# Seven filter outputs a block on all rows, and layer 0's convolution steps placed earlier, in a two-layer graph network kernel

## The chip, the cores and the metric

The kernel runs on one core of one Trainium2 chip. The metric is the device time of one execution in microseconds (us), as the median of several runs. "Span" below is the time from the first to the last instruction of the one execution that the profiler recorded.

## What is computed

For 64 graphs of 256 nodes with 256 features (all fp32), two layers run one after the other. Layer 0 has a convolution branch along the nodes, a message branch over the graph, and gates that mix both; layer 1 is a normalised aggregation.

```python
# layer 0, per graph
h = relu(bn1(conv1d(x^T, conv1_w, width 1)))
h = bn2(conv1d(h, conv2_w, width 17, pad 8))        # 256 -> 256 channels, 17 taps
x_conv = relu(h + x^T)^T
s = x @ w_se^T + b_se                                # 3 features
A = exp(-|s_n - s_m|^2) * adj
x_nmp = A @ relu(x @ w_msg^T + b_msg)
r, z, n = GRU gates of [x_conv, x_nmp] and x         # w_ih, w_hh
x = layernorm(x + (1 - z) * n + z * x)
# layer 1
h = layernorm(x) * gamma + beta
x = layernorm(x + x + relu((adj @ h) @ W_rel + b_rel + h @ W_root))
```

## The kernel before, in words

**Transform of the 17-tap convolution.** The node axis of a graph is cut into 16 stretches of 16, and two neighbouring stretches make a transform of length 32. VectorE (DVE in the profile) does the transforms as trees of two-input operations on the big tile `XF` (`fold` L789, `split` L607, `butterflies` L701, `merge` L640). Between them stands one complex product per frequency, done with three real 256x256 matrices on TensorE (PE). So the filter is needed as 47 real matrices (`NM`) of 256x256 instead of 17 taps.

**Filters (L523 to L592).** Those 47 matrices are made on the chip, once. The taps come from DRAM in pieces (`wt`, two buffers, L545). GpSimd (POOL) gathers the taps of a few outputs into a tile `ws` (L555, four buffers), TensorE turns it over (L562), ScalarE (ACT) copies the result out of PSUM to `tT` (L564), TensorE multiplies it with a constant matrix `taps` (L584), and ScalarE copies the product to its place in `W2` (L592). Before the change one block holds 3 outputs: 3 x 17 taps = 51 rows, product 128x141 (3 x 47). Two blocks lie one above the other in `ws` and `tT`, in rows 0 to 50 and 64 to 114, and the two products of such a pair use the two halves of the array's rows. A round has 6 blocks; there are 30 rounds, two of them with 2 blocks. That makes 172 products and 86 transposes, 60 gathers and 60 copies to `W2`.

**Batches and pairs.** The 64 graphs are 8 batches of 8. `conv1(b)` (L800) does for batch b, two graphs at a time, the load of x, its transposes (L841), the width-1 convolution (L862), and for b > 0 the store of the result to DRAM (`hd`, L871). `conv(b)` (L873) loads it back (L876), folds it (L795), splits it, does the products (`products`, L731; for b > 0 the matrices come from DRAM into the double-buffered `cs`, L724), merges, and leaves the convolved rows in `XC`. `pair(p)` (L1087) takes two graphs: messages (L1110), distances (L1143), aggregation (L1157), gates (L1195 for the first two pairs and the last one, L1209 with fewer products for the others), then the norm, projection (L1356) and aggregation (L1370) of layer 1, and the store.

**What sets the order.** All instructions are first recorded with a due time (`key`). `scheduled` (L316) then lays them out with a model of each engine's durations: at each step the ready instruction with the smallest key goes next on its engine. Keys of a pair count from `FIRST_GATES + p * PERIOD`; `spread` (L458) deals the steps of `filters`, `conv` and `conv1` evenly over a stretch of keys given by constants: `AHEAD_FROM, AHEAD_TO` for `conv1(1)`, `CONV1_FROM, CONV1_TO` for later `conv1`, `CONV_FROM, CONV_OUT, CONV_TO` for `conv`, `FILTERS_TO` for the filters. `PAIR_LEAD` makes the gates' DVE work more urgent than the convolution's. The keys only decide an order: on the chip each engine runs its own list in that order and waits by semaphores. All DMAs of the main part are issued by the SP queue, also in that order, so one that waits holds back those after it.

Of the kernel before, what the change touches and what calls it, by code (L numbers as in the profile page):

```python
# [18 lines left out]
P = 128  # L19
B, N, D = 64, 256, 256  # L20
C = D // P
TAPS, PAD = 17, 8
# [29 lines left out]
NM = 3 * len(LEAVES) + 2  # L52
SR, LR = 32, 100
SQ = 32
OB, OG = 3, 64
HQ = 2 * M * C * (M + 1)
XC_SLOTS = BG + 2
FIRST_GATES, PERIOD, GATE_TIME = 126, 59.2, 17.0
AHEAD_FROM, AHEAD_TO, W_DEEP = -20.0, 10.0, 2
CONV1_FROM, CONV1_TO, CONV_FROM, CONV_OUT, CONV_TO = -10.0, 120.0, -6.0, -58.0, -30.0  # L60
PAIR_LEAD, FILTER_LEAD, LOAD_AHEAD = 20.0, 15.0, 16.4
SMALL_RUNS, TURN_FROM = 1.3, 3
FILTERS_TO, STORES_AT = 50.0, 55.0
KEEP = 8.0
W_FROM, W_LAG = 2, 17.4
PLAIN, SUMS_FROM = (0, 1, B // 2 - 1), 2


# [101 lines left out]
class Op:  # L170

    def __init__(self):
        self.engine, self.calls, self.dur, self.moved, self.urgent = None, [], 0.0, 0, 0.0
        self.pre, self.post, self.spaces = set(), [], []


def one_line(line):
# [5 lines left out]
class Program:  # L183
# [13 lines left out]
    def add(self, name, method, args, named, line, reads, writes, dur, moved=0):  # L197
        op = self.joined
        if op is None or op.engine is None:
            op = op or Op()  # L200
            op.engine, op.key, op.seq = ENGINES[name], self.key, len(self.ops)
            self.key += self.step
            op.urgent = self.lead if op.engine == "DVE" else 0.0
            self.ops.append(op)
        op.calls.append((name, method, args, named, line))
        op.dur += dur
        op.moved += moved
        self.depend(op, reads, writes)
        return op

# [57 lines left out]
class Engine:  # L268
# [4 lines left out]
    def __getattr__(self, method):  # L273
        program, name = self.program, self.name

        def call(*args, hold=(), need=(), lines_up=0, **named):
# [12 lines left out]
            if method == "dma_start":  # L289
                v = outs[0] if isinstance(outs[0], View) else named["in_"]  # L290
                dur, moved = 0.06, v.size() * v.at.shape[0] * 4
                if program.joined is not None:
                    moved *= SMALL_RUNS
            elif name == "tensor":
# [21 lines left out]
def scheduled(ops):  # L316
# [4 lines left out]
    banks, held, queue = [0.0] * BANKS, {}, {}  # L321
    use, dma = dict.fromkeys(SHARES, 0), 0.0
    for op in ops:
        op.left, op.est = len(op.pre), op.key if op.engine == "SP" else 0.0
        for q in op.pre:
            q.post.append(op)
        for s in op.spaces:
            if s.where == "psum" and s.real is None and op.seq == s.ops[0].seq:
                s.left = {o.seq for o in s.ops}
                if s.line:  # L330
                    queue.setdefault(s.line, deque()).append(s)
# [83 lines left out]
def gnn_two_layers(  # L415
# [18 lines left out]
    prog = Program()  # L434
# [47 lines left out]
    xt_dram = tc.dram_tile([B // 2, P, C, 2 * N], F32, name="xt")  # L482
    w_dram = tc.dram_tile([2, SQ, 2 * C * C, P // SQ, P], F32, name="wd")
    W2 = sb("w2all", [P, C, NM, D], "first")
    taps = sb("taps", [P, NM * OB], "filters")

    prog.at(0.0)
    A.dma_start(out=chan_sb, in_=chan)
    A.dma_start(out=w1, in_=w1T.rearrange("(c p) n -> p c n", p=P))
    tb = np.zeros((2, OG, NM * OB), np.float32)  # L490
    tb[:, :TAPS * OB] = np.einsum("kf,op->kofp", tap_matrix(), np.eye(OB, dtype=np.float32)).reshape(TAPS * OB, NM * OB)
    tb = tb.reshape(P, NM * OB)
    A.dma_start(out=taps, in_=nc.inline_tensor(np.ascontiguousarray(tb), name="tap_matrix").ap())
    V.memset(mhalf, -0.5)
    V.memset(ones, 1.0)
# [25 lines left out]
            SP.dma_start(out=w2m[f:g, c].rearrange("f p o -> p f o"), in_=W2[:, c, f:g, :])  # L521

    def filters():  # L523
        pieces, rounds = [], []
        for c in range(C):
            for o0, o1 in ((0, 30 * OB), (30 * OB, 60 * OB), (60 * OB, D)):
                for o in range(o0, o1 - 6 * OB + 1, 6 * OB):
                    rounds.append((len(pieces), o, 3))
                if o1 == D:
                    rounds.append((len(pieces), D - 2 * OB, 1))  # L530
                pieces.append((c, o0, o1))
        WT, TT = {}, {}
        WS, AHEAD = {}, 4
        wts = ring("wt", [P, TAPS, 30 * OB], 2, "filters")
        wss = ring("ws", [P, 3, 2, OG], AHEAD, "filters")
        tTs = ring("tT", [P, 3, P], 2, "filters")
        for _ in range(AHEAD):
            G.memset(next(wss), 0.0)

        def fetch(i):  # L540
            if i < len(pieces):
                c, o0, o1 = pieces[i]
                t = next(wts).rearrange("p k o -> p (k o)")[:, :TAPS * (o1 - o0)]
                WT[i] = t.rearrange("p (k o) -> p k o", k=TAPS)
                SP.dma_start(out=WT[i], in_=w2T[c, :, :, o0:o1])  # L545

        def laid(i):
            piece, o, n = rounds[i]
            o -= pieces[piece][1]
            if i == 0 or rounds[i - 1][0] != piece:  # L550
                fetch(piece + 1)
            WS[i] = next(wss)
            for g in range(2):
                at = o + g * n * OB
                G.tensor_copy(WS[i][:, :n, g, :TAPS * OB].rearrange("p b (k o) -> p b k o", o=OB),  # L555
                              WT[piece][:, :, at:at + n * OB].rearrange("p k (b o) -> p b k o", o=OB))

        def turned(i):
            ps, n = bank("ps_tT"), rounds[i][2]
            with prog.group():  # L560
                for k in range(n):
                    PE.transpose(ps[:, k * P:(k + 1) * P], WS[i][:, k].rearrange("p g e -> p (g e)"), ident)  # L562
            tT = next(tTs)
            A.copy(tT[:, :n].rearrange("k b p -> k (b p)"), ps[:, :n * P])  # L564
            return tT

        fetch(0)
        for i in range(AHEAD):
            laid(i)
        TT[0] = turned(0)  # L570
        done = 0
        for i, (piece, o, n) in enumerate(rounds):
            c = pieces[piece][0]
            done = done if o else 0
            if i + AHEAD < len(rounds):
                laid(i + AHEAD)
            if i + 1 < len(rounds):
                TT[i + 1] = turned(i + 1)
            pss, size = [bank("ps_w") for _ in range(2)], NM * OB
            with prog.group():  # L580
                for k in range(n):
                    for g in range(2):
                        r = slice(g * OG, g * OG + TAPS * OB)
                        PE.matmul(pss[g][:, k * size:(k + 1) * size], TT[i][r, k, :], taps[r, :], start=k == 0,  # L584
                                  stop=k == n - 1, skip_group_check=True)
            for g in range(2):
                first = o + g * n * OB
                skip = max(0, done - first)
                done = first + n * OB
                pv = pss[g][:, :n * size].rearrange("p (b f o) -> p f b o", b=n, o=OB)  # L590
                to = W2[:, c, :, first:done].rearrange("p f (b o) -> p f b o", o=OB)
                A.copy(to[:, :, :, skip:], pv[:, :, :, skip:])  # L592

    def sl(a, n, step=1):
        return X[:, a:a + n] if step == 1 else X[:, a:a + (n - 1) * step + 1:step]
# [352 lines left out]
    prog.lead = 0.0  # L948
    at3 = len(prog.ops)
    spread(at1, at2, 2.0, 14.0)  # L950
    spread(at2, at3, 12.0, FILTERS_TO)
    for o in prog.ops[at1:at3]:
        if o.moved:
            o.key = min(o.key, 20.0)
# [41 lines left out]
    G.tensor_sub(half_r, half_r, bhh[:, 2])  # L996
    G.tensor_scalar(half_r, half_r, 0.5, None, ALU.mult)

    prog.at(STORES_AT, 0.01)
    store_w2(0)  # L1000
    store_w2(1)

# [519 lines left out]
```

## Time and profile before

| | |
|---|---|
| median of 3 runs | 2056.74 us (2054.84 to 2059.20) |
| profiled execution, own time | 2055.2 us |
| its span | 2053.4 us |
| mean granted TensorE clock | 0.985 of full |
| PE busy / weight loads / DVE / ACT / POOL | 2010.2 / 1632.0 / 1703.5 / 1033.2 / 310.4 us |

The span and what lies around it make up the profiled execution's own time, which is 1.5 us under the median. A matrix product in fp32 appears as two MATMUL records, a transpose as one, so a count of records on L584 is twice the count of products. Records of one engine overlap a little, so the pace of a run of them is read from start to start. The profile tells for each stretch the TensorE clock that was granted (PEclk, 1.00 is full), and for each wait the instruction that ended it.

### The profile page before, as it was taken

To read this page: it belongs to the slowest core of one execution; us is meant where nothing else is said; L and a number is where in the kernel's file an instruction comes from. 1 tells how busy PE (TensorE), PEld (TensorE's weight loads), DVE (VectorE), ACT (ScalarE), POOL (GpSimd) and SP (SyncE) were. 2 spreads that over 40 slices of the span, in tenths; PEclk is the share of its full clock that TensorE was granted. 3 is DMA by queue.
4 is the path that set the end of the run, shared out by engine and by line. 5 is a ranking of instruction groups with operands and counts; after the bars stand their busy time and mean duration, and the time that the engine had idled before them with its cause. 6 is when DMAs were issued, how large, how long until landed. Compare 5 with 4: busy or idle time off the path is not lost.

```text
span 2053.4 us, 28839 instructions
## 1 busy us (share of the span) xinstructions
PE 2010.2 (98%) x10332; PEld 1632.0 (79%) x10332; DVE 1703.5 (83%) x2611; ACT 1033.2 (50%) x2418; POOL 310.4 (15%) x564
## 2 busy tenths in 40 slices
PE   8999989999999999999999999999999999999996
PEld 6778778877887788878788788877888879877775
DVE  6685599899979999799989999799997999875644
ACT  5435533564446544464546553475444743565432
POOL 6410100111011112111110111111111110111000
PEclk8899999999999999999999999999999999999998
DMA  6744355435743465544654456544654336322100
GB/s 184 236 127 146 126 202 144 133 96 136 206 137 111 111 176 154 151 124 124 175 137 150 103 160 162 139 131 103 181 139 126 93 99 178 103 57 74 41 21 31
DMA packets 418590, 268.40 MB, mean 131 GB/s; under 512 B 217742, under 2 KB 403086, under 8 KB 418446
## 3 DMA queue, kind: packets, MB, share of 16 engines
q1 hardware_dynamic: 417886, 266.21, 45.3%
q8 instruction: 82, 1.34, 0.3%
q14 instruction: 62, 0.51, 0.1%
q10 hardware_dynamic: 560, 0.34, 0.1%
HBM read 191.39 MB, written 75.10 MB: 130 GB/s over the span
## 4 chain that ended last, share of the span: by engine, by line
PE 91%; DVE 6%; ACT 1%; DMA 1%; issue 1%; POOL 1%; SPq 0%; POOLq 0%; ACTq 0%; DVEq 0%
PE ps_a L1209 20%; PE ps_k L731 16%; PE ps_hy L1356 11%; PE ps_d L1209 10%; PE ps_agg L1370 5%; PE ps_msg L1110 5%; PE ps_nmp L1157 5%; PE ps_b L1209 5%; PE ps_c L862 5%; PE ps_g L1195 4%; PE ps_w L584 1%; PE ps_dist L1143 1%; POOL ws L555 1%; DVE XF L636 1%; DVE XF L634 1%
## 5 line engine op out<-in xcount | busy, mean ns | idle before, releaser
L731 PEld LDWEIGHTS ps_k<-XF,cs 128*128 128x128 f32 x2632 | 315.6, 193 | 21.3 <-DVE XF L703 8.0
L731 PE MATMUL ps_k<-XF,cs 128*128 128x128 f32 x2632 | 317.2, 276 | 7.1 <-DVE XF L703 7.1
L1356 PE MATMUL ps_hy<-wrr,wT 128*128 128x512 f32 x512 | 227.8, 596 | 0.0
L1209 PE MATMUL ps_a<-nmp,WB 128*128 128x256 f32 x696 | 207.0, 379 | 0.0
L1223 ACT ACTIVATE RG<-ps_a,bhh 128x512 f32<-128x512 f32 x116 | 79.4, 685 | 244.7 <-PE ps_a L1209 216.2
L1356 PEld LDWEIGHTS ps_hy<-wrr,wT 128*128 128x128 f32 x512 | 96.9, 191 | 108.7 <-issue 103.6
L1209 PE MATMUL ps_a<-tx,WB 128*128 128x256 f32 x522 | 156.3, 383 | 6.7 <-ACT RG L1223 6.7
L1209 PEld LDWEIGHTS ps_a<-nmp,WB 128*128 128x128 f32 x696 | 132.2, 190 | 18.0
L1110 PE MATMUL ps_msg<-wms,xT 128*128 128x260 f32 x512 | 133.3, 383 | 0.0
L1358 DVE SCALAR_TENSOR_TENSOR HY<-ps_hy,q,hrow 128x512 f32<-128x512 f32 x128 | 95.6, 748 | 44.3 <-PE ps_hy L1356 39.8
L703 DVE TENSOR_TENSOR XF<-XF 128x512 f32<-128x512 f32 (+3 forms) x128 | 127.3, 1007 | 4.8 <-ACT XF L784 3.0
L1370 PE MATMUL ps_agg<-HY,adja 128*128 128x256 f32 x512 | 120.4, 383 | 6.5 <-issue 6.5
L1370 PEld LDWEIGHTS ps_agg<-HY,adja 128*128 128x128 f32 x512 | 97.5, 192 | 32.9 <-issue 20.8
L1157 PE MATMUL ps_nmp<-AT,msg 128*128 128x256 f32 x512 | 118.2, 379 | 0.0
L1209 PEld LDWEIGHTS ps_a<-tx,WB 128*128 128x128 f32 x522 | 94.9, 190 | 27.2 <-ACT RG L1223 9.1
L1380 ACT ACTIVATE HY<-HY 128x256 f32<-128x256 f32 x112 | 46.2, 416 | 125.7 <-DVE HY L1374 125.7
L1157 PEld LDWEIGHTS ps_nmp<-AT,msg 128*128 128x128 f32 x512 | 96.2, 190 | 15.7 <-issue 2.4
L1221 ACT COPY ZN<-ps_a 128x512 f32<-128x512 f32 x116 | 67.6, 583 | 81.1 <-PE ps_a L1209 80.3
L862 PE MATMUL ps_c<-xTc,w 128*128 128x512 f32 x232 | 107.3, 594 | 0.8 <-ACT xTc L842 0.8
L1110 PEld LDWEIGHTS ps_msg<-wms,xT 128*128 128x128 f32 x512 | 95.1, 190 | 13.8 <-issue 1.3
L1209 PE MATMUL ps_a<-xc,WB 128*128 128x256 f32 x348 | 103.5, 379 | 0.0
L1209 PE MATMUL ps_d<-nmp,WB 128*128 128x256 f32 x348 | 103.5, 379 | 0.0
(209 smaller groups left out, 4401.2 us busy)
## 6 DMA issues: line engine op xcount, KB each, us to landing
cs<-w2m SPq DMA_DIRECT2D x105, 768.0 KB, 5.2
adjm<-in_adjT_dram SPq DMA_DIRECT2D x64, 256.0 KB, 3.0
xT<-xt SPq DMA_DIRECT2D x32, 512.0 KB, 3.7
adja<-in_adjT_dram SPq DMA_DIRECT2D x64, 256.0 KB, 2.9
out_dram<-HY SPq DMA_DIRECT2D x64, 256.0 KB, 2.2
hd<-xn SPq DMA_DIRECT2D x28, 544.0 KB, 3.3
XF<-hd SPq DMA_DIRECT2D x28, 544.0 KB, 3.9
xt<-xTc SPq DMA_DIRECT2D x29, 512.0 KB, 4.4
```

The source lines that it names most:

```text
L703: (V.tensor_add if add else V.tensor_sub)(sl(o, n), sl(a, n), sl(b, n))
L731: PE.matmul(ps[:, o * P:(o + 1) * P], w(m, c)[:, o * P:(o + 1) * P], X[:, slot, c * P:(c + 1) * P], start=first and o == 0 and c == 0, sto ...
L862: PE.matmul(ps, w1[:, c, o * P:(o + 1) * P], xTc[:, c, :], start=(c == 0), stop=(c == C - 1), hold=[h[:, :, o]])
L1110: PE.matmul(ps[:, :D + 4], xT[:, c, g, m * P:(m + 1) * P], wms[:, c, :], start=(c == 0), stop=(c == C - 1 and not idle), hold=[msg[:, g, m]])
L1157: PE.matmul(ps[:, d * N:(d + 1) * N], msg[:, g, m, d * P:(d + 1) * P], AT[:, g, m, :], start=(m == 0), stop=(m == C - 1), hold=[nmp[:, :, g]])
L1195: PE.matmul(ps[:, h * N:(h + 1) * N], block[:, s, gate, :], right[s][2 * k + g], start=0 in ks and h == 0 and s == sources[0] and k == 0, ...
L1209: PE.matmul(ps[:, h * N:(h + 1) * N], block[:, s, gate, :], right[s][at], start=start and h == 0 and j == 0, stop=j == len(sources) - 1, s ...
L1221: A.copy(o, ps)
L1223: A.activation(o, ps, AF.Identity, bias=bhh[:, 2, f:f + 1])
L1356: PE.matmul(ps, wT[:, 2 * f + g, m * P:(m + 1) * P], wrr[:, f, :], start=(f == 0), stop=(f == C - 1), hold=[HY[:, g, m]], need=[] if apart ...
L1358: stt(HY[:, g, m, :], ps, q[:, 1, j:j + 1], hrow)
L1370: PE.matmul(ps[:, n_ * D:(n_ + 1) * D], adja[:, g, m, n_ * P:(n_ + 1) * P], HY[:, g, m, :D], start=(m == 0), stop=(m == C - 1))
```

## The change

1. The filters go back to blocks of seven outputs: 7 x 17 = 119 rows in one block, no second block below it, product 128x329 (7 x 47). A group has up to four blocks; there are 20 groups (two of one block), 74 products and 74 transposes, 20 gathers of up to 476 elements a partition, 74 copies to `W2`. The four clearings of `ws` go. The taps come in pieces of 84, 84 and 88 outputs instead of 90, 90 and 76.
2. The constants of the due times change. `AHEAD_FROM, AHEAD_TO` go from -20, 10 to -57.8, -17.6, so that `conv1(1)`, the width-1 convolution of the second batch, stands ahead of the first pair's gates for three of its four graph pairs; `conv(1)` starts its folds right after the first batch's last merge step. `CONV1_TO` goes from 120 to 196.6. `FIRST_GATES`, `PERIOD`, `GATE_TIME`, `PAIR_LEAD`, `LOAD_AHEAD`, `KEEP`, `W_LAG` change by smaller steps.
3. In the planner, DMAs that write to DRAM no longer wait for their key, and the stores of the 47 matrices (`w2m`) are reckoned at 0.65 of their bytes.

The diff, cut to its core:

```diff
-OB, OG = 3, 64
+OB = 7
-FIRST_GATES, PERIOD, GATE_TIME = 126, 59.2, 17.0
-AHEAD_FROM, AHEAD_TO, W_DEEP = -20.0, 10.0, 2
-CONV1_FROM, CONV1_TO, CONV_FROM, CONV_OUT, CONV_TO = -10.0, 120.0, -6.0, -58.0, -30.0
-PAIR_LEAD, FILTER_LEAD, LOAD_AHEAD = 20.0, 15.0, 16.4
+FIRST_GATES, PERIOD, GATE_TIME = 124.4, 58.2, 16.7
+AHEAD_FROM, AHEAD_TO, W_DEEP = -57.8, -17.6, 2
+CONV1_FROM, CONV1_TO, CONV_FROM, CONV_OUT, CONV_TO = -10.0, 196.6, -6.0, -57.1, -31.9
+PAIR_LEAD, FILTER_LEAD, LOAD_AHEAD = 31.8, 15.0, 22.3
-FILTERS_TO, STORES_AT = 50.0, 55.0
-KEEP = 8.0
-W_FROM, W_LAG = 2, 17.4
+KEEP = 7.7
+W_FROM, W_LAG = 2, 20.1
...
+                if not isinstance(outs[0], View) and outs[0].tensor.name.startswith("w2m"):
+                    moved *= 0.65
...
-        op.left, op.est = len(op.pre), op.key if op.engine == "SP" else 0.0
+        op.left, op.est = len(op.pre), op.key if op.engine == "SP" and not op.stores else 0.0
...
-    taps = sb("taps", [P, NM * OB], "filters")
+    taps = sb("taps", [TAPS * OB, NM * OB], "filters")
...
-            for o0, o1 in ((0, 30 * OB), (30 * OB, 60 * OB), (60 * OB, D)):
+            for o0, o1 in ((0, 12 * OB), (12 * OB, 24 * OB), (24 * OB, D)):
...
-        wss = ring("ws", [P, 3, 2, OG], AHEAD, "filters")
-        tTs = ring("tT", [P, 3, P], 2, "filters")
-        for _ in range(AHEAD):
-            G.memset(next(wss), 0.0)
+        wss = ring("ws", [P, 4, TAPS, OB], AHEAD, "filters")
+        tTs = ring("tT", [TAPS * OB, 4, P], 2, "filters")
...
-            for g in range(2):
-                at = o + g * n * OB
-                G.tensor_copy(WS[i][:, :n, g, :TAPS * OB].rearrange("p b (k o) -> p b k o", o=OB),
-                              WT[piece][:, :, at:at + n * OB].rearrange("p k (b o) -> p b k o", o=OB))
+            G.tensor_copy(WS[i][:, :n], WT[piece][:, :, o:o + n * OB].rearrange("p k (b o) -> p b k o", o=OB))
...
-                    for g in range(2):
-                        r = slice(g * OG, g * OG + TAPS * OB)
-                        PE.matmul(pss[g][:, k * size:(k + 1) * size], TT[i][r, k, :], taps[r, :], start=k == 0,
-                                  stop=k == n - 1, skip_group_check=True)
-            for g in range(2):
...
-                A.copy(to[:, :, :, skip:], pv[:, :, :, skip:])
+            for a, o in enumerate(starts):
+                ps = bank("ps_w")
+                PE.matmul(ps[:, :NM * OB], TT[i][:, a, :], taps, start=True, stop=True)
+                skip = OB - D % OB if o == D - OB else 0
+                pv = ps[:, :NM * OB].rearrange("p (f o) -> p f o", o=OB)
+                A.copy(W2[:, c, :, o + skip:o + OB], pv[:, :, skip:])
...
-    spread(at2, at3, 12.0, FILTERS_TO)
+    spread(at2, at3, 12.0, 70.0)
...
-    prog.at(STORES_AT, 0.01)
+    prog.at(58.0, 0.01)
```

## The prediction

> **What bounds the kernel now.** I read the page's head first, then the time by stages, then the waits of TensorE, and last the chain of work around the longest wait.
>
> ```profile
> span 2053.4 us, 28839 instructions
> PE 2010.2 (98%) x10332; PEld 1632.0 (79%) x10332; DVE 1703.5 (83%) x2611; ACT 1033.2 (50%) x2418; POOL 310.4 (15%) x564
> ```
>
> PE is busy for all but 43 us, so time can be had only from PE's work, from its few gaps, and from stretches with a lower clock. The stages show where those lie (columns: stretch, its length, then busy us and records of PE, PEld, DVE, ACT, POOL, then PEclk, DMA share, GB/s):
>
> ```profile
> 24.00:28.00 4.00, 4.00 (x38) 2.79 (x37) 2.40 (x4) 3.25 (x8) 1.58 (x3) 1.00 0.55 134
> 28.00:32.00 4.00, 2.13 (x22) 1.52 (x19) 3.97 (x4) 1.93 (x5) 4.00 (x4) 1.00 0.79 171
> 36.00:40.00 4.00, 3.99 (x32) 3.65 (x34) 3.93 (x6) 2.28 (x6) 3.74 (x7) 0.50 0.87 198
> 56.00:60.00 4.00, 1.50 (x17) 1.09 (x15) 3.96 (x2) 2.37 (x6) 4.00 (x2) 1.00 0.02 4
> 68.00:72.00 4.00, 4.00 (x24) 3.07 (x26) 3.90 (x6) 2.73 (x6) 1.80 (x4) 0.50 1.08 384
> 260.00:270.00 10.00, 2.87 (x13) 2.42 (x12) 9.79 (x11) 1.03 (x2) 0.00 (x0) 0.78 0.30 110
> ```
>
> In the filter stage PE runs out of work twice while POOL is fully busy, and after each gap its clock is halved for a long time. The third place is at 260 us. Its chain (start us, us, what):
>
> ```profile
> 225.67 3.45 PE ps_c L862 x8
> ...
> 230.23 4.38 DMA hd<-xn
> ...
> 235.06 4.86 DMA XF<-hd
> ...
> 239.95 2.50 DVE XF L795 x4
> ...
> 265.24 2.30 DVE XF L703
> ```
> ```profile
> PE ps_k L731 <- DVE XF L703: 7.1, 1, 7.1
> PE ps_tT L562 <- POOL ws L555: 6.1, 5, 2.7
> ```
>
> The last graph pair of conv1(1) leaves PE at 229.1. It goes through DRAM, is folded, and is split by DVE without a pause until 267.5. PE has by then done all else that its list holds, and waits 7.1 us.
>
> **What the Trainium skill says.** *TensorE: Matmul & The Clock Gate*, Part 1: the array's clock is halved after an idle window of about 3.4 us and comes back after a busy one. The trace agrees that a gap halves it, but not that a busy window restores it: from 36 to 44 us PE is busy throughout with the 51-row products and stays at 0.50. After the gap at 260, the 128-row products have the full clock again by 280. The same page, Part 3: products on separate row groups run side by side. The trace agrees: six products of 141 columns take 0.92 us, 0.153 each, where one after the other would take at least 0.25 (two records of 0.124, the pace of the 128-column ps_k). *SBUF — State Buffer*, "two separate sides": a DVE operation with two SBUF inputs and a GpSimd operation hold the shared port for a whole instruction, and the other waits. The trace agrees: the L555 copy takes 0.334 us while DVE is idle (13.6 to 15.9), and in median 1.326 beside DVE operations of 1.24 to 1.36 us (26.4 to 33.6).
>
> **Part 1, the filters.** Before, the stage goes from the first product to the first ps_k: 24.82 to 85.59, 60.8 us. These lines of PE's timeline give its paces:
>
> ```profile
> 24.82 0.99 PE L584 MATMUL ps_w<-taps,tT 51*128 51x141 f32 x12
> 25.74 0.55 PE L562 MATMUL ps_tT<-ident,ws 128*128 128x128 f32 x3
> 26.22 0.99 PE L584 MATMUL ps_w<-taps,tT 51*128 51x141 f32 x12
> ...
> 63.62 1.78 PE L584 MATMUL ps_w<-taps,tT 51*128 51x141 f32 x12
> 65.34 0.90 PE L562 MATMUL ps_tT<-ident,ws 128*128 128x128 f32 x3
> ```
>
> Start to start, six products take 0.92 us and three transposes 0.48 at full clock, 1.72 and 0.83 at half. At full clock the stage holds 172 x 0.153 = 26.4 and 80 transposes (six are done earlier) x 0.16 = 12.8, together 39.2 us. The other 21.6 us are about 7 of waits (6.1 for POOL, 0.8 for tT) and about 15 of halved clock.
>
> After: a product of 329 columns is not in the trace. Records of 256 columns come every 0.216 us (eight in 1.73, L1157), of 512 every 0.431 (eight in 3.45, L862). Between them, 329 gives 0.277, two records 0.555; 74 make 41.1 us. As a lower end by columns alone from the 512 pace it is 41.0, as an upper end by the step from 128 (0.124) to 256 it is 41.9. Twelve transposes stand ahead of the stage in the new order, six more than before (1.0 us), and 62 x 0.16 = 9.9 remain. In all 52.0 us: PE does 12.8 us more work, and loses 21.6 of waits and slow clock. **Gain 8.8.**
>
> This needs covers. POOL: 20 gathers instead of 60. Each waits at most for one DVE operation (0.7 to 1.36 us, 2.35 for three of them) and takes between 0.6 (a fixed part of 0.2 and the rest by elements) and 1.04 us (0.334 x 476/153); 1.36 + 1.04 = 2.4 lies under PE's 2.86 for a group (4 x 0.555 + 4 x 0.16), and four buffers carry the three long ones. ACT: four copies of 329 at no more than the 0.541 of 423 elements, and one of 512 at 0.594: 2.76, under 2.86 too. The pieces of taps, 714 KB, land in 5 to 8 us and are asked for two groups or more ahead. If a cover fails and one slow stretch like those of 13.7 and 20.5 us comes back, it costs 7 to 10; I take none and keep +10 for the range. Below 52 lies only what the transposes may overlap, about 1 us.
>
> What comes next is not late: DVE ended its first splits at 78.8, and I take the same after; ps_k would start at 79 to 80 (a half group of conv1(1) now stands before it), and the first eight groups of products need only the parts done by 65.
>
> **Part 2, conv1(1) ahead of the gates.** One graph pair costs PE 0.88 + 3.43 = 4.3 us, moved, not added: 0. Its DMAs move too. On SP, the 12 loads of the gates' weights (WB) now stand behind the third pair's xt store, which waits for that pair's transposes. Their issue took 8.4 us before (141.4 to 149.8). From those transposes to the first gate PE has 10.9 us (one ps_k group 0.99, L862 3.43, three messages at 1.51, L1063 1.92); ACT's two copies, the store and the first six loads need 1.2 + 0.5 + 4.2, and about 2.5 to land. That fits by 2.5 us; cost 0, at worst 3.
>
> What it buys is at 260. In the new order PE has 9.5 us of work from the last conv1(1) pair to the last gate product of pair 0, and then 44.0 us up to the first ps_k of batch 1: 48 gate products at 0.432 (20.7), L1356 6.9, L862 5.2, L1370 3.5, four messages 3.5, transposes 2.6, L1157 1.7. That is 53 us where the chain took 38.5. But DVE's list puts the split behind pair 0's gate steps: 8 us of those, 25 of splits at the durations of 242 to 267, 7 of msg, hy and agg operations between them: 40 us against 44, and 42 with the waits for hy and msg that I count on the way. So PE should not wait, with 2 us in hand. What goes: 7.1 (ps_k), 1.3 and 0.3 (x loads and xTc just before and after), 0.7 (ps_wT at 295), and the halved clock, in which 48 ps_k records took 7.9 us instead of 5.9: 11.4. **I take 10**, as late x loads may stay; bounds 2 (the wait stays, shorter) and 11.
>
> **Part 3, all later work.** The counts of instructions from batch 1 on are the same, and the last 477 PE instructions stand in the same order, so the gaps of the end (about 16 us) stay. Between 300 and 1900 nearly the whole order differs. PE idles there 9 us in all; I take 0 for the change, bounds -5 and +8. The unkeyed stores cost nothing: the DMAs are busy 0.4 to 0.6.
>
> **Sum.** 2055.2 - 8.8 - 10 = 2036.4 for an execution like the profiled one. That one ran 1.5 under the median of 2056.7, so 2037.9; I say **2038**.
>
> **Rivals.** (B) The filter stage gains nothing: POOL is again late or the clock stays halved for some 20 us; for it, the slow clock did outlast full PE work; against it, there are a third of the gathers and 119 rows at work. 2056.7 + 1 - 10 = 2048. (C) The wait at batch 1 only moves, as DVE's list has 2 us in hand: 2056.7 - 8.8 = 2048. (D) **Slower**: later batches now find what batch 1 found at 260. The place is the first ps_k of a batch; the price 10 us each (7.1 of wait and about 3 of clock and follow-up). DVE is at 90 to 93% in most hundreds from 300 to 1800, and the new order deals conv1 over a longer stretch (to 196.6), so the last load may come later before the split. Against it, before has no such wait after 300. It decides from the second batch on; three make 2038 + 30 = 2068.
>
> **Chances.** Forecast 0.55, B 0.13, C 0.10, D 0.22. The forecast's own range is 2029 to 2048; with B and C nearly 0.8 lies there, and I reach up to 2058 for the lighter cases of D. Faster by over 0.2% (4.1 us, about what a measurement can tell from none): all of the forecast, most of B and C, 0.74. Within: 0.07. Slower: 0.19.
>
> **What would show it.** Right: in the stages from 25 to 80 PEclk 1.00, POOL waits of ps_tT under 1 us, the first ps_k near 80; no wait of ps_k for L703 (line moved by 16) above 2 us near 240 to 250. Wrong: PEclk 0.50 in the filter stage, ps_w records further apart than 0.28, or new ps_k waits for DVE after 300.

## The result, and the profile after

The changed kernel takes **2020.51 us** (median of 4 runs, 2019.95 to 2020.71), against 2057.46 for the kernel before (4 runs, 2054.84 to 2059.20). The ratio is 0.9821, with a 95% interval of 0.9804 to 0.9838. The forecast was 2038, in a range of 2029 to 2058: the sign is right, and the gain is twice what was forecast. A later measurement gave 2020.25 (2019.92 to 2020.76).

The head of the page after has fewer PE records (the filters), the same DVE work, and a PE that is idle for 20 us of its span instead of 43:

```profile
span 2018.8 us, 28419 instructions
PE 1998.5 (99%) x10124; PEld 1623.3 (80%) x10124; DVE 1703.6 (84%) x2611; ACT 1036.9 (51%) x2422; POOL 290.3 (14%) x520
```

The stages that were shown of before, in the kernel after (columns: stretch, its length, then busy us and records of PE, PEld, DVE, ACT, POOL, then PEclk, DMA share, GB/s):

```profile
28.00:32.00 4.00, 4.00 (x18) 2.89 (x17) 3.97 (x4) 3.66 (x9) 0.95 (x1) 1.00 0.93 215
36.00:40.00 4.00, 4.00 (x18) 2.86 (x17) 3.93 (x6) 3.49 (x8) 3.74 (x6) 1.00 0.61 140
56.00:60.00 4.00, 4.00 (x21) 2.99 (x20) 3.96 (x3) 3.48 (x9) 4.00 (x3) 1.00 1.03 335
68.00:72.00 4.00, 4.00 (x22) 2.99 (x21) 3.83 (x8) 3.62 (x9) 0.04 (x1) 1.00 0.06 19
260.00:270.00 10.00, 10.00 (x77) 9.59 (x76) 9.74 (x14) 5.22 (x11) 0.31 (x2) 1.00 0.70 246
```

PE is busy in every one, at the full clock. Even from 56 to 60 us, where POOL is busy throughout as it was in the gaps of before, PE goes on from `ws` buffers that were filled earlier. The gap at 260 is gone.

PE's timeline in the filter stage after (start us, us, engine, line, what):

```profile
34.69 0.60 PE L556 MATMUL ps_tT<-ident,ws 128*119 128x128 f32 x4
35.13 2.38 PE L573 MATMUL ps_w<-taps,tT 119*128 119x329 f32 x8
```

Four transposes take 0.44 us from start to start, 0.11 each. The forecast had them at 0.16.

Of PE's waits in the kernel after, these two lines are the largest (us in total, times, longest). The first stands in the last 20 us and is the same before and after:

```profile
PE ps_agg L1354 <- issue: 6.5, 1, 6.5
PE ps_a L1193 <- ACT RG L1207: 1.3, 2, 0.7
```

In the kernel before, the second one came six times between 478 and 1846 us, and the prediction did not price it:

```profile
PE ps_a L1209 <- ACT RG L1223: 6.7, 6, 2.8
```

**Where the time went.** For every PE record I take the time to the next record's start, less the median of that time for its kind over all kernels of this study. What is left over in a stretch is PE's excess: its waits and its slow clock. In the filter stage I take the whole time of transposes and products instead. With the start and the last 80 us added (1 to 4 and 9.4 to 9.7 us of excess, not shown), these columns add up to the differences in span within 0.7 us for every kernel. Only differences between rows count: the level of a column depends on how finely records are sorted into kinds, and part of it is no wait at all. Each row is one profiled run.

| us | filters | to 150 | 150-295 | 295-1800 | 1800-1940 | span |
|---|---|---|---|---|---|---|
| before | 60.8 | 2.6 | 13.2 | 11.2 | 5.6 | 2053.4 |
| after | 47.8 | 1.5 | 1.1 | 5.2 | 3.3 | 2018.8 |
| e1 filters alone | 47.8 | 1.8 | 9.9 | 17.0 | 3.2 | 2040.5 |
| e9 = e1 + AHEAD | 47.8 | 2.2 | 2.2 | 16.3 | 3.2 | 2031.1 |
| e11 = e9 + CONV1_TO | 47.8 | 2.2 | 1.3 | 10.7 | 3.1 | 2025.5 |
| e13c = e11 + pair times | 47.8 | 2.1 | 5.6 | 12.9 | 6.2 | 2035.0 |
| e2 after, old filters | 56.7 | 2.5 | 5.6 | 4.7 | 6.2 | 2038.5 |
| e3 after, old AHEAD | 47.8 | 4.9 | 5.2 | 4.9 | 6.2 | 2029.5 |
| e7 after, old pair times | 47.8 | 2.7 | 2.1 | 8.5 | 3.0 | 2024.4 |
| e8 after, old CONV1_TO | 47.8 | 1.5 | 0.6 | 15.6 | 6.2 | 2032.1 |
| e5 e2, one gather a round | 46.7 | 3.4 | 0.9 | 5.2 | 1.4 | 2022.3 |
| e10 e5, taps ahead of stores | 40.8 | 1.6 | 1.5 | 4.8 | 3.3 | 2013.9 |
| e12b e10, rounds in twos | 37.6 | 5.0 | 13.0 | 9.8 | 4.5 | 2030.6 |

(After the filters' column, "to 150" counts from the first ps_k; e2 and e5 also have slow conv1 products among the filters, 0.9 and 4.5 us.) From before to after, 13.0 us come out of the filters, about 13 out of the stretch from there to 295, and about 8 from later.

### The profile page after: what moved, and what is told of

The parts are those of the page before. It is cut to its first block, busy times and chain, and to the rows that moved or that the text cites. A ratio compares the mean times of both kernels' runs of the same rounds, so it can differ in the third digit from the quotient of the medians.

```text
span 2018.8 us, 28419 instructions
## 1 busy us (share of the span) xinstructions
PE 1998.5 (99%) x10124; PEld 1623.3 (80%) x10124; DVE 1703.6 (84%) x2611; ACT 1036.9 (51%) x2422; POOL 290.3 (14%) x520
## 4 chain that ended last, share of the span: by engine, by line
PE 97%; DVE 1%; ACT 1%; issue 1%; POOL 0%; DMA 0%; ACTq 0%; POOLq 0%; DVEq 0%
PE ps_a L1193 22%; PE ps_k L715 16%; PE ps_d L1193 11%; PE ps_hy L1340 11%; PE ps_agg L1354 6%; PE ps_msg L1094 6%; PE ps_c L846 5%; PE ps_b L1193 5%; PE ps_nmp L1141 5%; PE ps_g L1179 4%; PE ps_w L573 2%; PE ps_dist L1127 1%; PE ps_xTc L825 0%; PE ps_tT L556 0%; PE ps_sT L1118 0%
## 5 line engine op out<-in xcount | busy, mean ns | idle before, releaser
L1193 PE MATMUL ps_a<-tc,WB 128*128 128x256 f32 x348 | 103.5, 379 | 0.0
```

The source lines that it names most:

```text
L1193: PE.matmul(ps[:, h * N:(h + 1) * N], block[:, s, gate, :], right[s][at], start=start and h == 0 and j == 0, stop=j == len(sources) - 1, s ...
```

## The experiments

### e1: the filters alone

The kernel before with the seven-output filter code, every due time and the planner as before.

```diff
-OB, OG = 3, 64
+OB = 7
...
```

> The kernel before with the seven-output filters alone; all due times and the planner as before. Theory (three parts that add: filters 13, conv1 ahead of the gates 13, later waits 8.5 us): 2044 (2041 to 2047), PEclk 1.00 from 25 to 75 us, and the wait of ps_k for the S butterfly of batch 1 still there with 7 us or so. Rival (the filter stage's gain is lost again, since batch 1's chain through DRAM and DVE, not PE, sets the time up to its first product): 2053 or more, with the wait of batch 1 longer by what the filters won.

Measured: 2041.97 us (2041.15 to 2043.96), ratio to before 0.9919 (0.9905 to 0.9934). The clock is 1.00 in the whole stage, and TensorE waits for no gather. The stage takes 47.8 us. The two other losses stay (PE's waits in e1; for the second one, the wait for the first product of the second batch, the profile finds no releaser and says "issue"):

```profile
PE ps_a L1191 <- ACT RG L1205: 8.6, 7, 2.8
...
PE ps_k L713 <- issue: 6.0, 1, 6.0
```

So the filters alone are worth about 13 to 18 us: 13.0 in their own stage, 12.9 between the spans of the profiled runs, 15.5 between the medians, and 18.0 against the kernel before as it was measured beside e1 (2059.97). They remove neither the wait at the second batch, which falls from 7.1 to 6.0, nor the waits for RG, which rise from 6.7 to 8.6.

### e2: the due times alone

The kernel after with the three-output filters of before.

```diff
-OB = 7
+OB, OG = 3, 64
...
```

> The kernel after with the three-output filters of before; due times and planner as after. Theory: 2034 (2031 to 2037): the POOL waits and the halved clock of the filter stage are back (13 us), no wait at batch 1, few waits later. Rival (conv1's steps fill the gaps of the filter stage, so the due times carry nearly all of the gain): under 2025, PEclk above 0.9 in the filter stage.

Measured: 2039.85 us (2038.55 to 2046.36), ratio 0.9915 (0.9891 to 0.9938), so 19.3 over the kernel after. The wait at the second batch is gone and the halved clock in the filters is back; the time lies 3 us above the theory's range. Three stretches of e2:

```profile
40.00:50.00 10.00, 9.48 (x77) 8.25 (x73) 9.83 (x15) 7.76 (x18) 9.24 (x13) 0.58 0.39 106
...
62.20:72.20 10.00, 9.98 (x58) 7.86 (x60) 9.66 (x16) 4.60 (x10) 7.00 (x12) 0.50 1.03 340
72.20:76.20 4.00, 3.57 (x45) 2.85 (x45) 3.86 (x9) 3.37 (x8) 0.00 (x0) 1.00 1.03 291
```

From 62.2 to 72.2 PE does nothing but rounds of the old filters, without a pause, at the halved clock; then the clock is back, with the same rounds going on. By the table 8.9 of the 19.3 are in the filters' own records, and 0.9 in conv1's products among them. The others are mostly waits at new places (3.3 for sts at 165 us, 2.1 of ps_nmp at 1913), with a halved clock after each. This is the first sign that what happens later depends on the whole order, and not on the constant that was edited.

### e3: conv1(1) back at the gates

```diff
-AHEAD_FROM, AHEAD_TO, W_DEEP = -57.8, -17.6, 2
+AHEAD_FROM, AHEAD_TO, W_DEEP = -20.0, 10.0, 2
```

> The kernel after with only the due times of the second batch's conv1 back at the first pair's gates (-20 to 10). Theory: the wait of batch 1's first product for DVE's S butterfly comes back with 5 to 9 us and a halved clock after it: 2031 (2028 to 2034). Rival (the other constants, which place DVE's split and gate steps, removed that wait): 2020 to 2022, no such wait.

Measured: 2030.96 us (2028.24 to 2031.63), ratio 0.9862 (0.9847 to 0.9877), 10.4 more than the kernel after. The size is that of the theory, the named wait isn't there: in place of one long wait of ps_k there are ps_nmp for AT (6.1 us in 3 waits, two of them before 260 us) and ps_msg for a load (1.5, with the clock at 0.83 from 80 to 90). 7.5 of the 10.4 lie before 295, the rest at 1898 to 1906.

### e4: PAIR_LEAD back

```diff
-PAIR_LEAD, FILTER_LEAD, LOAD_AHEAD = 31.8, 15.0, 22.3
+PAIR_LEAD, FILTER_LEAD, LOAD_AHEAD = 20.0, 15.0, 22.3
```

> The kernel after with only PAIR_LEAD back at 20, so that the gates' DVE steps are less urgent against the convolution's. Theory: the waits of ps_a for ACT's RG copy, which itself waits for DVE's last use of RG (six of 0.75 to 3 us between 470 and 1850 in the kernel before, two after), come back: 2026 (2023 to 2029). Rival (the later waits went with another constant, the period or conv1's longer stretch): 2020 to 2021, no more than three such waits.

Measured: 2020.08 us (2019.61 to 2020.57), ratio 0.9812 (0.9797 to 0.9826). The waits for RG stay at 1.2 us. My theory that the greater urgency of the gates' DVE work removed them fell here.

### e5: old filters, one gather a round

The three-output blocks in e2 were starved by two GpSimd instructions a round. Here one gather fills both halves. Two things go with it: the copies to `W2` take every second block, and the planner now places a transpose only where its buffer `tT` is free (`hold`).

```diff
-            for g in range(2):
-                at = o + g * n * OB
-                G.tensor_copy(WS[i][:, :n, g, :TAPS * OB].rearrange("p b (k o) -> p b k o", o=OB),
-                              WT[piece][:, :, at:at + n * OB].rearrange("p k (b o) -> p b k o", o=OB))
+            G.tensor_copy(WS[i][:, :n].rearrange("p b g e -> p (b g) e")[:, :, :TAPS * OB].rearrange("p j (k o) -> p j k o", o=OB),
+                          WT[piece][:, :, o:o + 2 * n * OB].rearrange("p k (j o) -> p j k o", o=OB))
...
-                    PE.transpose(ps[:, k * P:(k + 1) * P], WS[i][:, k].rearrange("p g e -> p (g e)"), ident)
+                    PE.transpose(ps[:, k * P:(k + 1) * P], WS[i][:, k].rearrange("p g e -> p (g e)"), ident, hold=[tT])
...
```

> The changed kernel with the three-output blocks of before, but each round is gathered by one GpSimd instruction instead of two (the two blocks of a pair are now neighbours, the copies to W2 take every second block). Products and transposes are the same in number as in e2 (172 and 86), GpSimd gathers 30 instead of 60. Theory (GpSimd's second instruction in a round waits behind a VectorE operation, which starves TensorE, and the gaps halve the clock): PEclk near 1.00 from 25 to 80 us, no ps_tT wait for GpSimd above 1 us, and the stage shrinks to some 40 to 45 us (26.4 of products, about 3 of transposes at 0.11 after the first, and about 0.35 of drains in each of 30 rounds): 2039.9 of e2 less 15 to 20, 2018 to 2025, level with the changed kernel. Rival (products on 51 rows cannot keep the clock up whatever feeds them): the clock is halved again for some 30 us and the time stays at 2035 to 2041.

Measured: 2024.26 us (2019.35 to 2024.64), ratio 0.9840 (0.9817 to 0.9863). The clock is 1.00 up to 68 us, so 51-row products do keep it up as long as they are fed. In the filter stage PE's waits for `tT` fall from 3.2 us (e2) to 0.3, which may be due to `hold`; the two edits were not tried apart. What is left is one long wait for a gather:

```profile
PE ps_tT L563 <- POOL ws L555: 4.5, 2, 4.1
```

GpSimd isn't the cause of this one: it is idle from 54 to 68.9, waiting for the last piece of the taps. SP's queue in e5 shows why that is late:

```profile
45.83 12.76 SPq L523 DMA_DIRECT2D w2m<-w2all  x6
58.69 2.67 SPq L547 DMA_DIRECT2D wt<-in_w2T_dram  x1
```

Six stores stand ahead of the load on SP and take 12.8 us to issue (they no longer wait for their due time). After the gap:

```profile
74.00:78.00 4.00, 4.00 (x28) 3.13 (x26) 3.90 (x8) 1.80 (x5) 0.00 (x0) 0.50 0.15 53
...
82.00:84.00 2.00, 2.00 (x11) 2.00 (x11) 0.00 (x0) 0.00 (x0) 0.00 (x0) 0.50 0.96 272
84.00:86.00 2.00, 2.00 (x15) 2.00 (x15) 0.00 (x0) 0.27 (x1) 0.00 (x0) 0.71 0.54 123
```

The clock is halved from 68.1 to 85.1 us: 10.9 us of uninterrupted filter work from 69.6 to 80.5 did not restore it, and it came back 4.6 us after the 128-row ps_k products had begun.

### e6: a gap made on purpose in the new filters

In the kernel after, one gather is done 16 times (the same values).

```diff
-            G.tensor_copy(WS[i][:, :n], WT[piece][:, :, o:o + n * OB].rearrange("p k (b o) -> p b k o", o=OB))
+            for _ in range(16 if i == 11 else 1):
+                G.tensor_copy(WS[i][:, :n], WT[piece][:, :, o:o + n * OB].rearrange("p k (b o) -> p b k o", o=OB))
```

> The changed kernel with one of GpSimd's gathers done 16 times over (the same values), which starves TensorE once in the middle of the filter stage for some 5 to 12 us. It tells what brings the clock back after a gap. Theory (products on 119 rows at a time are work enough for the clock, products on 51 rows are not): the clock falls to 0.50 in the gap and is 1.00 again within about 7 us of TensorE's return. Rival (any fp32 product of this stage leaves it halved, it is the later 128-row products of ps_k that restore it): 0.50 for 13 us or more after the gap, as in before and in e5. The time rises by the gap and half of the slow stretch, 2027 to 2040, and is not what is asked for.

Measured: 2036.27 us (one run). The stages around the gap, in e6:

```profile
54.00:56.00 2.00, 0.00 (x0) 0.00 (x0) 1.97 (x3) 0.00 (x0) 1.88 (x3) 1.00 1.04 350
...
58.00:60.00 2.00, 1.65 (x4) 1.21 (x5) 1.93 (x3) 0.44 (x2) 2.00 (x3) 0.50 1.03 337
60.00:62.00 2.00, 2.00 (x8) 1.52 (x7) 2.00 (x1) 1.22 (x3) 2.00 (x1) 0.67 1.04 345
```

PE is back at 56.9, the clock is at 0.50 from 57.9 to 61.3, and at 1.00 from then on. A gap of the same kind costs 3.4 us of half clock here, against 13.7 and 20.5 in before, 10.2 and 13.7 in e2, 17.1 in e5. The theory holds in this one run with its one long gap: the new stage recovers within 3.4 us. The old one recovers too, but takes 10 us and more. What decides was not separated: the rows at work (119 or 51), the changes between products and transposes (below), or the share of transposes, which is 0.83 of the 2.54 us of an old round at the halved clock and, at the full clock, 0.44 of the 2.66 of a new group.

### e10: the taps ahead of the stores

e5, with the stores held to their key on SP so that the last piece of the taps goes first.

```diff
-        op.left, op.est = len(op.pre), op.key if op.engine == "SP" and not op.stores else 0.0
+        op.left, op.est = len(op.pre), op.key if op.engine == "SP" and (not op.stores or 50.0 <= op.key < 50.2) else 0.0
...
-    prog.at(58.0, 0.01)
+    prog.at(50.0, 0.01)
```

> e5, with one edit in the planner and one key: the stores of the 47 matrices wait for their key again, so that on SP the last piece of the taps (asked for at 58.7 us in e5, behind six stores, and landed at 68.9) is issued ahead of them. Theory: nothing then starves TensorE in the filter stage; PEclk is 1.00 up to the first ps_k, the gap of 7 us and the 17 us of halved clock behind it (68.0 to 84.6) go, the last filter product ends near 66 instead of 80, and the kernel takes 2024.3 - 14 = 2010, ahead of the changed kernel by 10. Rival: VectorE's first splits, which end near 81 in e5, are the next thing that is late, TensorE waits in ps_k for XF between 66 and 81, and what is won in the filters is mostly lost there: 2017 to 2022.

Measured: **2014.19 us** (2014.02 to 2017.37), ratio to before 0.9794 (0.9779 to 0.9808). All its runs lie below all those of the changed kernel (2019.92 to 2020.76), by 6 us in the median. The two were not run side by side; of the ratios to the kernel before, e10's upper end (0.9808) lies just above the lower end of the changed kernel's first measurement (0.9804) and just below that of its second (0.9811). The clock is 1.00 throughout the stage, and its filters take 40.8 us, 7.0 less than the seven-output blocks:

```profile
60.00:70.00 10.00, 9.46 (x93) 6.88 (x90) 9.80 (x10) 9.62 (x23) 5.33 (x3) 1.00 1.04 349
```

VectorE's splits, the rival, did not hold ps_k back. The forecast of 2010 was 4 too low: of the 14 us, 12.0 came (5.9 in the filters, 4.3 in conv1's products among them, 1.8 just after), but 1.5 were given back ahead of the first product and 1.9 between 1800 and 1940. PE's timeline in e10 gives the pace of a round:

```profile
30.83 0.99 PE L584 MATMUL ps_w<-taps,tT 51*128 51x141 f32 x12
31.75 0.55 PE L563 MATMUL ps_tT<-ident,ws 128*128 128x128 f32 x3
32.23 0.99 PE L584 MATMUL ps_w<-taps,tT 51*128 51x141 f32 x12
```

A round takes 1.40 us. Record by record, a transpose between two transposes takes 0.109, but the last one ahead of a product 0.202; a pair of product records, one for each half of the array, takes 0.120, but the first pair of a round 0.224 and the last 0.217. Three times 0.11 and six pairs at 0.12 give 1.05, so 0.35 us a round go to the two changes. In the kernel after, where products and transposes alternate too, but the products work on 119 rows, a change costs next to nothing: the first transpose takes 0.113 and the last 0.108, the first product record 0.281 and the last 0.277.

### e12 and e12b: rounds in twos

e10 with six transposes and then twelve products, so half as many changes. The work is the same.

```diff
             with prog.group():
-                for k in range(n):
-                    PE.transpose(ps[:, k * P:(k + 1) * P], WS[i][:, k].rearrange("p g e -> p (g e)"), ident, hold=[tT])
+                for j in two:
+                    for k in range(rounds[j][2]):
+                        PE.transpose(pss[j][:, k * P:(k + 1) * P], WS[j][:, k].rearrange("p g e -> p (g e)"), ident,
+                                     hold=[TT[j]])
...
-        for i, (piece, o, n) in enumerate(rounds):
+        for i in range(0, len(rounds), 2):
+            two = [j for j in (i, i + 1) if j < len(rounds)]
...
```

> e10 with the filter rounds taken in twos: six transposes, then twelve products, instead of three and six, so that TensorE changes between transposes on the whole array and products on half its rows 15 times each way instead of 30. The numbers of products, transposes and copies are the same; tT has four buffers. Theory (each change drains the array: in e10 a round of three transposes and six products takes 1.397 us, where the paces inside the runs, 0.11 and 0.12, give 1.05, so 0.35 a round): a pair of rounds takes 2.45 instead of 2.79 us, the stage shrinks by about 5 and the time is 2009 (2008 to 2011). Rival (ScalarE's three copies a round, 1.39 us from start to start in e10, set the pace, and what looks like a drain is TensorE held back by them): no gain, 2013 to 2016, and waits of ps_tT or ps_w for ScalarE's copies appear.

Measured: 2034.38 us (2031.93 to 2036.04), ratio 0.9884 (0.9870 to 0.9899), 20 more than e10 and outside both forecasts. e12b is the same kernel with a trace.

> The kernel of e12 once more, for its trace: it took 2034.4 us, 20 more than e10, where both theories had said 2008 to 2016. A third theory: the doubled groups wait for PSUM banks, since four products' banks and two for transposes are held at once and come free only by ScalarE's copies; then TensorE waits for ScalarE in ps_tT or ps_w each round and the gaps halve the clock. A fourth: GpSimd's gathers, now needed two at a time with the same four buffers, are late; then ps_tT waits for GpSimd. A round inside an undisturbed stretch still tells whether doubling saves the 0.35 us.

Measured: 2032.67 us (one run). PE's timeline in e12b:

```profile
27.71 1.71 PE L591 MATMUL ps_w<-taps,tT 51*128 51x141 f32 x24
29.35 0.87 PE L566 MATMUL ps_tT<-ident,ws 128*128 128x128 f32 x6
30.16 1.71 PE L591 MATMUL ps_w<-taps,tT 51*128 51x141 f32 x24
```

Two rounds take 2.45 us instead of 2.79: the 0.35 us are there, and ScalarE's copies did not set the pace. The filters take 37.6 us in spite of 3.3 us of waits for GpSimd (part of the fourth theory), so the stage did what was forecast. The loss is all behind it: in the table the stretches from the first ps_k to 1940 have 32.3 us of excess, against 11.2 in e10, above all a wait of 6.8 us of ps_wT for DVE's wT from 184 us, after which the clock stays halved until 200.5. The order of the later work came out worse, although only the filters had been edited.

### e8, e9 and e11: CONV1_TO undone, AHEAD added, CONV1_TO added

e8 is the kernel after with this edit:

```diff
-CONV1_FROM, CONV1_TO, CONV_FROM, CONV_OUT, CONV_TO = -10.0, 196.6, -6.0, -57.1, -31.9
+CONV1_FROM, CONV1_TO, CONV_FROM, CONV_OUT, CONV_TO = -10.0, 120.0, -6.0, -57.1, -31.9
```

> The changed kernel with the later conv1 dealt over the short stretch of before alone (CONV1_TO 120). Theory 2 (with conv1 packed into the first half of a batch's time, TensorE runs into ps_a earlier against VectorE in the second half, and waits for RG): 5 to 9 us of waits of ps_a for RG come back, 2026 to 2030. Theory 1 (the pairs' distance did it): at most 2 us of these waits, 2019 to 2022. Theory 3: in between.

Measured for e8: 2033.46 us (2031.92 to 2034.05), ratio 0.9888 (0.9863 to 0.9913), 13 more than the kernel after. The waits of theory 2 are back, at a higher cost than it forecast (2026 to 2030); five of them stand 239 us apart, one a batch:

```profile
PE ps_a L1193 <- ACT RG L1207: 9.1, 8, 2.8
```

> e1 (before with the seven-output filters alone, 2042.0) and AHEAD_FROM, AHEAD_TO at -57.8, -17.6 in addition, nothing else of the change. Theory (the conv1 of the second batch ahead of the gates is worth the whole of what the trace lost at 225 to 300, 13 us): no wait of ps_k of 6 us near 245, 2029 with 1.5 either way; the waits of ps_a for RG in later batches stay at 6 to 9 us, which are the remaining 8. Rival (the wait at the second batch only goes with the other times as well, CONV_OUT and the pairs' times): 2036 to 2042.

Measured for e9 (e1 with AHEAD_FROM, AHEAD_TO at -57.8, -17.6): 2031.85 us (2030.61 to 2035.34), ratio 0.9885 (0.9863 to 0.9908), 10.1 less than e1. The wait at the second batch goes with AHEAD alone; the waits for RG stay:

```profile
PE ps_a L1191 <- ACT RG L1205: 8.9, 6, 2.8
```

> e9 (before with the seven-output filters and AHEAD, 2031.9) and CONV1_TO at 196.6 in addition. Theory (the longer stretch for conv1 is what takes the later waits away, as its undoing in e8 brought nine of them back): ps_a waits for RG 3 us at most instead of 8.9, the excess of TensorE between 295 and 1940 us falls by 6 to 9 us, time 2023 (2021 to 2026), which leaves at most 5 for all other constants. Rival (it needs the other constants, LOAD_AHEAD or the pairs' times, beside it): the waits stay above 6 us and the time at 2029 or more.

Measured for e11 (e9 with CONV1_TO at 196.6): 2029.65 us (2027.15 to 2032.38), ratio 0.9870 (0.9850 to 0.9890). The waits for RG fall as the theory said:

```profile
PE ps_a L1191 <- ACT RG L1205: 2.1, 2, 1.5
```

But the median falls by 2 us only, which the intervals do not tell from nothing. The four runs are two near 2027 and two near 2032; the profiled one is of the faster two, so the table's 5.6 us from e9 to e11 show e11 at its best. New waits take part of the gain back: ps_msg waits 3.1 us for a load at 1587, ps_nmp 1.9 at 438.

### e7 and e13c: the pairs' due times, undone and added

e7 is the kernel after with this edit:

```diff
-FIRST_GATES, PERIOD, GATE_TIME = 124.4, 58.2, 16.7
+FIRST_GATES, PERIOD, GATE_TIME = 126, 59.2, 17.0
```

> The changed kernel with the pairs' due times of before alone (FIRST_GATES 126, PERIOD 59.2, GATE_TIME 17.0). Open is which constant took the waits of ps_a for RG (6.7 us and a halved clock of 1.8 in before, 8.6 in e1) away from the later batches; PAIR_LEAD has fallen. Theory 1 (the pairs' distance: a pair's gates now begin at another place against the convolution's VectorE work): the waits come back to 5 to 9 us and the time to 2026 to 2030. Theory 2 (the stretch over which conv1 is dealt, CONV1_TO): this one stays at 2019 to 2022 with at most 2 us of these waits. Theory 3 (no one constant, each order has its own luck): some waits in between, 2 to 5 us, 2021 to 2025.

Measured for e7: 2026.68 us (2026.09 to 2027.22), ratio 0.9857 (0.9837 to 0.9878), 6.2 more than the kernel after, with 4.4 us of waits for RG. The waits are those of theory 3, the time is above its range.

> e11 (before with the seven-output filters, AHEAD and CONV1_TO, 2029.7) and the pairs' due times of the changed kernel (FIRST_GATES 124.4, PERIOD 58.2, GATE_TIME 16.7) in addition. In e11 the waits for RG have gone, but a wait of ps_msg for the xT load at 1587 (3.1 us), one of ps_nmp at 438 (1.9) and one for RG at 1639 (1.6) stand there instead. Theory 1 (the pairs' times take these away, as their undoing in e7 brought back 4.4 of waits for RG and cost 6 us): 2022 to 2025, with under 3 us of such waits between 295 and 1800. Rival (they are the luck of each order, and other constants decide as much): such waits of 3 us or more stay at this or another place, 2026 to 2031.

Measured for e13c (e11 with the pairs' times of the kernel after): 2036.01 us (2034.33 to 2036.88), ratio 0.9900 (0.9880 to 0.9920). So the same constants that are worth 6 us inside the changed kernel cost 6 on top of e11. The waits for RG are at 0.9, and another wait has taken their place:

```profile
PE ps_d L1191 <- DVE nmp L1160: 4.7, 2, 3.6
```

The rival holds, with a time above its range: no sum of single constants explains the later stretches.

### e14b: the kernel after once more

> The changed kernel itself once more, on the chip of this call, for the spread between chips and calls: 2019.5 to 2021.5.

Measured: 2020.25 us, ratio 0.9826 (0.9811 to 0.9842).

## Why the prediction was right and wrong

**Part 1, the filters: right mechanism, a term mis-sized.** Forecast 8.8, measured 13.0 in the stage (60.8 to 47.8). The clock stayed at 1.00, the covers held, and the price of 0.277 for a 329-column record was met: 74 products took 41.0 us, 41.1 forecast. What failed is the price of a transpose. "62 x 0.16 = 9.9": they took 6.8, 0.11 each, and the 1.0 for six more of them ahead of the stage hardly showed (the first product starts at 24.95 instead of 24.82). "Three transposes in 0.48" had been read off as the price of a transpose, but 0.15 of that 0.48, and 0.2 of the 0.92 of the six products, are the changes between half-array products and full-array transposes, which the new code doesn't have. The Trainium skill names a cause that fits, on the page *TensorEngine Tiling (Array Packing)*, Key Properties: changing the tiling mode drains the engine. It gives no price; e10 shows 0.35 us a round, e12b shows it saved when the changes are halved, and the kernel after shows no such cost where the products use the whole array. So fed work on the old blocks is 40.8 us (e10, with 1.2 of waits in it; the forecast had 39.2), on the new 47.8 (52.0). The new code costs 7.0 us more of work and not 12.8, and saves 20.0 of waits and slow clock, for which 21.6 had been forecast.

**Part 2, conv1(1) ahead of the gates: right.** Forecast 10, with 11.4 listed. The wait of ps_k is gone, and neither the queue of WB loads nor a late x load cost anything that shows. AHEAD undone costs 10.4 (e3) and alone brings 10.1 (e9 on e1). That both are so near to 10 is in part luck: of the 10.4 some 3 lie at 1898 to 1906, and the wait that e3 was to bring back did not come; of the 10.1 the table shows 7.7 in the stretch from 150 to 295. From before to after this stretch fell by 12.1, of which the filters alone take 3.3 (e1).

**Part 3, all later work: wrong, and the main miss.** "PE idles there 9 us in all; I take 0 for the change, bounds -5 and +8" put a term at nothing without a reason. The excess from 295 to 1940 fell by 8.3 us (16.8 to 8.5). Idle time and clock say the same: in before PE idles 9.5 us there and loses 1.7 to a halved clock, in after it idles 2.8 and loses nothing. By medians, what is left after the filters (15.5) and AHEAD (10.1) is 11.3. The stretch in before and in after:

```profile
295.00:1940.00 1645.00, 1635.47 (x8316) 1338.62 (x8315) 1446.45 (x2194) 853.85 (x2048) 232.25 (x427) 1.00 0.47 132
```
```profile
295.00:1940.00 1645.00, 1642.21 (x8298) 1344.10 (x8298) 1432.31 (x2186) 859.38 (x2047) 231.45 (x429) 1.00 0.47 130
```

Of the 9.5 us, 6.7 are six waits of ps_a for RG that the profile of before lists. Here is the longest of them in the timeline of before (start us, us, engine, line, what, and in brackets how long the engine had been idle and for whom):

```profile
1662.35 1.22 DVE L1283 TENSOR_TENSOR RG<-xT,ZN 128x1024 f32<-128x1024 f32 x1
...
1663.60 1.23 DVE L1284 SCALAR_TENSOR_TENSOR RG<-ZN,RG 128x1024 f32<-128x1024 f32 x1
1664.86 1.23 DVE L1285 SCALAR_TENSOR_TENSOR wT<-ZN,RG 128x1024 f32<-128x1024 f32 x1
...
1666.18 0.69 ACT L1223 ACTIVATE RG<-ps_a,bhh 128x512 f32<-128x512 f32 x1 [4.98 <-DVE wT L1285]
...
1666.92 0.70 PE L1209 MATMUL ps_a<-tx,WB 128*128 128x256 f32 x2 [2.81 <-ACT RG L1223]
```

RG has one buffer. The next pair's first copy into it waits for the three DVE steps that still use the old one, and ps_a waits for the copy. So PE waits wherever it comes to ps_a before DVE is through. Shown by the runs: with CONV1_TO at 120 (before, e1, e8, e9) these waits are 6.7 to 9.1 us, with 196.6 (twelve profiles) 0.9 to 4.4. That conv1's PE work, dealt over a longer stretch, keeps PE from running ahead in the second half of a batch fits the 239 us between the waits of e8, but is only argued. What takes their place (loads, nmp, AT) differs from kernel to kernel: with CONV1_TO at 196.6 the excess between 295 and 1800 runs from 4.7 to 12.9 us, and e12b and e13c show that it can't be assigned to single constants. Which of the other constants gives the changed kernel its low 5.2 stays open.

**The rivals.** B (nothing gained in the filters) and C (the wait only moves) fell with the trace after. D, slower by new waits at the first ps_k of later batches, didn't happen: ps_k waits nowhere in the kernel after by more than 0.3 us. "The unkeyed stores cost nothing" held for the changed kernel, but not with the old filters, where six of them kept the last taps back (e5). D's worry, that a new order brings new waits of several us later on, is what e12b and e13c did, at other instructions. The range was too narrow on the low side because part 3 was priced at nothing, where the trace had up to 11.2 us to be won.

## What to carry to other kernels

Read an instruction's price from records in the middle of a run of its kind; at the ends it contains what the change of mode costs, and that term goes or comes with the pattern. When a planner lays out the whole program, price a change of its constants by the waits that the present order has (here 9.5 us behind 295, and 1.7 of slow clock), and expect that an edit can redraw them, here by anything from nothing (e4) to 20 us (e12b). A starved stage is worth a look at who starves it before it is replaced: one gather in place of two (with `hold`), and one load ahead of six stores, made the old filters 7 us faster than the new ones, and the kernel 6 us faster than the changed one.

## What the runs showed of the hardware

- A change between transposes on the whole array and products on half its rows and back costs 0.35 us together (1.397 us a round in e10, 2.445 for two rounds in e12b), spread over the records on both sides. Between transposes and products on 119 rows there is no such cost (after).
- The halved clock after a gap lasted 3.4 us under 119-row products (e6), and 10.2 to 20.5 us under rounds of 51-row products and transposes (before, e2, e5), although TensorE was busy throughout for 10.9 us of it in e5 and for 10.0 in e2, after which it came back in e2. Old filters are not the only case: in e12b the clock stayed halved for 13.7 us from 186.9, where TensorE, back from its wait at 190.8, did mostly transposes up to 195, with two more short waits. The page *TensorE: Matmul & The Clock Gate* of the Trainium skill, Part 1, lets one busy window of about 3.4 us suffice; e6 agrees, e2 and e5 don't. The rounds of the old filters keep a full clock once they have it (e10, from 27 to 68 us).
- 329 columns in fp32 take 0.277 us a record, between the 0.216 of 256 columns and the 0.431 of 512.
